# Score pieces in pairs, batch exponentials and separate message tiles in two edge-attention loops

## The chip, the cores and the metric

The kernel runs on one core of a Trainium2 chip. The time is the device time of one execution in microseconds (us); the kernel before has a median of 6476.23 us over four runs (6473.66 to 6476.97). A core has five engines with an instruction stream each: TensorE (PE, matrix products), VectorE (DVE), ScalarE (ACT), GpSimd (POOL) and SyncE (SP). Here POOL issues the gathers (indirect DMAs, one row of a table for each of 128 partitions) and SP the plain DMAs.

## The reference, cut to what matters

A graph network with two attention layers, each followed or preceded by dense layers:

```python
x = x + gat(layernorm(x))             # 6250 nodes, 206250 edges, 4 heads of 64
x = x + mixture_of_experts(layernorm(x))
x = x + weighted_neighbour_sum(layernorm(x))
x = x + gat_routed_ffn(layernorm(x))  # 131072 edges, 4 heads of 4, then 4 experts
# both attentions, for each edge (src, dst) and each head:
e = leaky_relu(a_src[src] + a_dst[dst], 0.2)
p = exp(e - segment_max(e, dst)[dst])
out = segment_sum(p / segment_sum(p, dst)[dst] * h[src], dst)
```

Both attentions run through one function, `gat_stream`. Edges are sorted by destination.

## The kernel before

**Tiles, pieces, batches.** 128 edges, one per partition, make an edge tile. Q = 8 edge tiles make a piece, PB = 4 pieces (B = 32 edge tiles) a batch. The first attention has 1612 edge tiles, that is 202 pieces (the last has 4 tiles) in 51 batches; the second has 787, that is 99 pieces (the last has 3) in 25 batches. `DH` is the width of a message (256 and 16), `H` = 4 the heads, `W = DH + 2 * H`. `parts` is 1 in the first attention and 3 in the second, where messages are split into three bf16 terms. `s.group` is 16 in the first and None in the second.

**One loop, written out by hand.** `gat_stream` ends with a loop over steps `s_` under a manual schedule: instructions stand on each engine in the order in which the loop writes them, and each engine takes its own in order. In step `s_` with `k = s_ - 2` and `q = s_ - 10` the loop writes:

- `gathers(s_)` (L1303): eight indirect DMAs on POOL, one for each edge tile, into a tile `g` of the piece, which holds the message part h[src] and a_src[src]. Of these tiles there are 13 in the first attention and 14 in the second.
- `load(s_ + 3)` (L1279, L1285), every fourth step: the destinations of a batch, spread over all partitions (`db`, two tiles of 8 KB a partition), and the marks `kf` of where a destination starts. On SP.
- what is left of earlier nodes: `done` (L1974 to L1994 in the first attention), then `normed`, `twice`, `logits` in later steps.
- `scores(k)` (L1333 to L1343): DVE sums three terms of a_dst (`nd`, from a PSUM tile `pds` with two halves, one for even and one for odd pieces), adds a_src out of `g`, takes the leaky relu, subtracts the node's own score and writes `Z`. The add is the first instruction that waits for the gathers of piece k to land.
- `turned_hots(k + 3)` (L1313): DVE compares `db` with the node numbers; `node_parts(k + 2)` (L1324): PE picks a_dst with it, into the half of `pds` that `scores(k)` has just read.
- `greatest`, `turn_scores`, `turn_back` once a batch: two scans on DVE (L1355, L1358) find the greatest score of each destination, PE turns the tile before and after.
- `weights(i)` (L1374 to L1379), once a batch, when `k % 4 == 3`: ACT takes the exponentials of the whole batch into `ps[0]`; then, for each of the four pieces, ACT takes them again into columns DH to DH + H of the piece's `g`, and DVE writes the product of the maximum and the end mark `il` into the last H columns.
- `one_hots(q + 1)` (L1184) and `messages(q + 1)` (L1386): DVE multiplies the message part by the exponentials, in place in `g`. In the second attention it then makes the three bf16 terms (L1391, L1393).
- `sums(q, 0)` and `sums(q, 1)` (L1409): PE adds up the messages of each destination; it reads `g` itself in the first attention, which frees the tile of piece q at step q + 10.

**Around it.** The first attention's result goes to a routed layer whose expert products (L634, L647) fill the middle of the span; the weighted neighbour sum with its own gathers (L234) follows; the second attention comes last, and the kernel ends with its last nodes.

## Time and profile before

| what | value |
|---|---|
| median of four runs | 6476.23 us |
| profiled execution, its own time | 6479.13 us |
| its span | 6477.3 us |
| first attention's gathers, first issue to last end | 192.87 to 2241.08 us |
| weighted sum's gathers (L234) | 1616 of 947 ns |
| second attention's gathers, first issue to last end | 5390.06 to 6394.25 us |
| PE, DVE, ACT, POOL busy over the span | 59%, 67%, 19%, 63% |

Busy shares over the whole span mix stages with different limits; what a change in one stage is worth is read in a window of that stage. In a line of the timeline, the first number is the start in us and the second the duration; what stands in square brackets is how long the engine was idle before, and what ended the wait. A group's line ends with busy time, mean duration of one in ns, and the idle time before its instructions with what ended it. "issue" means that the engine waited for nothing that the profile shows.

### The profile page before, as it was taken

To read this page: it belongs to the slowest core of one execution; us is meant where nothing else is said; L and a number is where in the kernel's file an instruction comes from. 1 tells how busy PE (TensorE), PEld (TensorE's weight loads), DVE (VectorE), ACT (ScalarE), POOL (GpSimd) and SP (SyncE) were. 2 spreads that over 40 slices of the span, in tenths; PEclk is the share of its full clock that TensorE was granted. 3 is DMA by queue.
4 is the path that set the end of the run, shared out by engine and by line. 5 is a ranking of instruction groups with operands and counts; after the bars stand their busy time and mean duration, and the time that the engine had idled before them with its cause. 6 is when DMAs were issued, how large, how long until landed. Compare 5 with 4: busy or idle time off the path is not lost.

```text
span 6477.3 us, 61956 instructions
## 1 busy us (share of the span) xinstructions
PE 3819.2 (59%) x17583; PEld 2863.5 (44%) x17583; DVE 4330.1 (67%) x10445; ACT 1204.2 (19%) x2770; POOL 4094.1 (63%) x4304
## 2 busy tenths in 40 slices
PE   4266666666666679999514777776777677111111
PEld 3144444444445458888402444444444445111111
DVE  5266666666666683444368888888888872777777
ACT  2011111112221112333100222222222222000000
POOL 0677777777777612232147777777777765777773
PEclk9678777778877789999755888888888888555555
DMA  4644555554545425557563444444444443233332
GB/s 131 142 146 145 146 147 147 146 146 146 146 145 146 112 97 196 187 185 235 182 213 112 128 126 129 129 128 125 129 128 127 126 118 83 53 76 76 76 76 56
DMA packets 495996, 856.25 MB, mean 132 GB/s; under 512 B 140311, under 2 KB 345304, under 8 KB 486135
## 3 DMA queue, kind: packets, MB, share of 16 engines
q0 software_dynamic: 190112, 461.21, 26.8%
q1 hardware_dynamic: 280226, 366.94, 17.3%
q10 hardware_dynamic: 25300, 24.00, 1.1%
q8 instruction: 143, 2.34, 0.2%
q14 instruction: 215, 1.75, 0.1%
HBM read 758.44 MB, written 95.50 MB: 132 GB/s over the span
## 4 chain that ended last, share of the span: by engine, by line
POOL 33%; DVE 18%; issue 17%; PE 16%; DMA 15%; ACT 1%; DVEq 0%; SPq 0%; ACTq 0%; POOLq 0%; another core or an unknown queue 0%
POOL g L234 17%; POOL g L1303 16%; DMA g<-tab,si 7%; PE py L647 5%; PE ph L634 5%; DMA g<-tab_ef,si 3%; DVE g L1386 3%; DVE run L2102 3%; PE acc L1409 2%; DMA g<-tab_1f,si1s 2%; DVE oh L1184 2%; DMA xc<-x_d 1%; DVE ot L1313 1%; PE bacc L1435 1%; DVE R L1355 1%
## 5 line engine op out<-in xcount | busy, mean ns | idle before, releaser
L234 POOL DMA_INDIRECT g<-tab_ef,si x1616 | 1530.9, 947 | 618.6 <-issue 590.5
L1303 POOL DMA_INDIRECT g<-tab,si x1612 | 1557.4, 966 | 505.1 <-issue 411.9
L2102 DVE SCALAR_TENSOR_TENSOR run<-g,wab,run 128x256 f32<-128x256 f32 x2626 | 1264.1, 488 | 328.1 <-DMA g<-tab_ef,si 248.5
L1409 PE MATMUL acc<-g,oh 128*128 128x264 f32 x3224 | 1013.9, 468 | 309.5 <-DVE g L1386 242.8
L1409 PEld LDWEIGHTS acc<-g,oh 128*128 128x128 f32 x3224 | 726.3, 234 | 492.5 <-DVE g L1386 272.2
L1303 POOL DMA_INDIRECT g<-tab_1f,si1s x787 | 764.6, 972 | 250.3 <-issue 213.3
L2219 PE MATMUL acc<-run,oh 128*128 128x256 f32 x808 | 302.5, 511 | 689.7 <-DVE oh L2106 534.0
L1335 DVE TENSOR_TENSOR z<-g,nd 128x32 f32<-128x32 f32 (+1 forms) x301 | 58.0, 193 | 841.9 <-DMA g<-tab,si 687.9
L1409 PE MATMUL acc<-s,oh 128*128 128x72 bf16 x1267 | 106.4, 249 | 751.5 <-DVE s L1391 751.5
L2219 PEld LDWEIGHTS acc<-run,oh 128*128 128x128 f32 x808 | 190.3, 251 | 792.6 <-issue 468.5
L1772 PE MATMUL pf<-xt,w 128*128 128x512 f32 (+1 forms) x832 | 410.9, 627 | 98.5 <-ACT h L1777 98.4
L1386 DVE TENSOR_TENSOR g<-g,mix 128x2048 f32<-128x2048 f32 x202 | 458.9, 2272 | 0.0
L1409 PEld LDWEIGHTS <-oh 128*128 128x128 bf16 x1267 | 85.8, 127 | 763.1 <-issue 480.6
L1784 PE MATMUL pf<-w,h 128*128 128x256 f32 x1568 | 403.4, 401 | 0.0
L634 PE MATMUL ph<-xe,w 128*128 128x256 f32 x1664 | 377.1, 383 | 4.9 <-DVE xe L622 4.9
L647 PE MATMUL py<-w,h 128*128 128x256 f32 x1664 | 370.0, 380 | 0.0
L610 POOL DMA_INDIRECT xg<-tab_x,gi x104 | 117.8, 1133 | 351.9 <-PE pt L619 278.6
L634 PEld LDWEIGHTS ph<-xe,w 128*128 128x128 f32 x1664 | 316.7, 192 | 48.3 <-DVE xe L622 5.9
L1784 PEld LDWEIGHTS pf<-w,h 128*128 128x128 f32 x1568 | 289.7, 195 | 100.3 <-issue 67.0
L647 PEld LDWEIGHTS py<-w,h 128*128 128x128 f32 x1664 | 312.4, 191 | 40.1
L650 POOL DMA_INDIRECT tab_y<-y,so x104 | 111.9, 1076 | 267.9 <-DVE y L649 263.4
L1772 PEld LDWEIGHTS pf<-xt,w 128*128 128x128 f32 x832 | 164.2, 210 | 247.8 <-issue 124.4
(510 smaller groups left out, 6076.4 us busy)
## 6 DMA issues: line engine op xcount, KB each, us to landing
w<-in_L_ffn_W SPq DMA_DIRECT2D x104, 1024.0 KB
db<-s_d SPq DMA_DIRECT2D x74, 1024.0 KB
yb<-y_d SPq DMA_DIRECT2D x49, 640.0 KB
g<-tab_ef,si POOLq DMA_INDIRECT x1616
g<-tab,si POOLq DMA_INDIRECT x1612
y_d<-y SPq DMA_DIRECT2D x196, 128.0 KB
g<-tab_1f,si1s POOLq DMA_INDIRECT x787
yy<-tab_y SPq DMA_DIRECT2D x7, 1792.0 KB
```

The lines of the kernel that those rows point to most:

```text
L234: nc.gpsimd.indirect_dma_start(out=dst, out_offset=None, in_=table, in_offset=bass.IndirectOffsetOnAxis(ap=si[:, t:t + 1], axis=0))
L610: nc.gpsimd.indirect_dma_start(out=xg[:, i, :], out_offset=None, in_=tab_x, in_offset=bass.IndirectOffsetOnAxis(ap=gi[:, 2 * j + i:2 * j + ...
L634: nc.tensor.matmul(ph, w1[:, k, f * P:(f + 1) * P], xe[:, k, :], start=(k == 0), stop=(k == KD - 1))
L647: nc.tensor.matmul(py, hs[f][:, i * P:(i + 1) * P], w2[:, f, :], start=(f == 0), stop=(f == FC - 1))
L1184: nc.vector.tensor_tensor(o[:, :m], ips[:, None, k * P:(k + 1) * P].to_broadcast([P, m, P]), dl[:, a:a + m, None].to_broadcast([P, m, P]), ...
L1303: nc.gpsimd.indirect_dma_start(out=g[:, j, :DH + H], out_offset=None, in_=tab, in_offset=bass.IndirectOffsetOnAxis(ap=si[:, t0 + j:t0 + j ...
L1386: nc.vector.tensor_mul(gh, gh, ps[0][:, o:o + n, :, None].to_broadcast([P, n, H, CD]))
L1409: nc.tensor.matmul(acc[b].rearrange("p s w -> p (s w)"), oh[:, t - a], m_, start=(t == lo), stop=(t == hi))
L1772: nc.tensor.matmul(ph[:, :n], w1[:, e, k, f * P:(f + 1) * P], xts[g][:, k, :n], start=(k == 0), stop=(k == KD - 1))
L1784: nc.tensor.matmul(py[:, :D], hs[g, e, f][:, j * P:(j + 1) * P], w2[:, e, f, :], start=False, stop=(f == FC - 1))
L2102: nc.vector.scalar_tensor_tensor(at[:, i] if j < Q - 1 else r[i], g[:, j, :], w, at[:, i], op0=OP.mult, op1=OP.add)
L2219: nc.tensor.matmul(acc[i], oh[:, k], r[k], start=(q % 2 == 0 and k == 0), stop=(last and k == 1))
```

## The change

- **Messages of the first attention.** `g` loses the columns for the maxima (260 columns in place of 264) and has 11 tiles in place of 13. `messages` writes the product into a new tile `m` (264 columns, 3 tiles), an ACT copy puts the exponentials and maxima into its last 8 columns, and `sums` reads `m`. The tile `g` is so free after `messages`, at step q + 9.
- **Exponentials and maxima of a batch.** `weights` makes one exponential and one DVE product for the whole batch, in a tile `pw`. In the second attention four ACT copies a batch bring them into the pieces; in the first, the copies in `messages`.
- **Scores for two pieces.** At even k, `scores` takes pieces k - 1 and k together: one reduction over both halves of `pds`, an add for each piece, one leaky relu, a subtraction for each piece. A last piece that is not full is taken alone, and so is the piece before it in that step.
- **Order.** `turned_hots` runs two pieces ahead in place of three and `node_parts` one in place of two. In the first attention `load` brings two pieces at a time (`LB = 2`, 4 KB a partition, still two tiles), so that `load(q)` has to wait until `turned_hots(q - 3)` has read the tile.

```diff
--- before.py
+++ after.py
@@ -1236,6 +1236,7 @@
         PB = B // Q
         nbatch = -(-npiece // PB)
         LAG = 10
+        LB = 2 if s.group else PB
         with ExitStack() as st:
             pool = lambda name, bufs, **k: st.enter_context(tc.tile_pool(name=f"{s.name}_{name}", bufs=bufs, **k))
             gp = pool("gs", 1)
@@ -1273,11 +1274,11 @@
                 return Z[i]
 
             def load(q):
-                if q % PB == 0:
-                    n = min(PB * Q, T - q * Q) * P
-                    d = mp.tile([P, PB * Q * P], I16, name="db", bufs=2)
+                if q % LB == 0:
+                    n = min(LB * Q, T - q * Q) * P
+                    d = mp.tile([P, LB * Q * P], I16, name="db", bufs=2)
                     nc.sync.dma_start(d[:, :n], s.d16[q * Q * P:q * Q * P + n][None, :].to_broadcast([P, n]))
-                    for k in range(PB):
+                    for k in range(LB):
                         dbs[q + k] = d[:, k * Q * P:(k + 1) * Q * P]
                 if q % PB == 0:
                     i = q // PB
@@ -1298,7 +1299,7 @@
 
             def gathers(q):
                 t0, n = span(q)
-                g = piece[q] = mp.tile([P, Q, W], F32, name="g", bufs=13 if parts == 1 else 14)
+                g = piece[q] = mp.tile([P, Q, DH + H if parts == 1 else W], F32, name="g", bufs=11 if parts == 1 else 14)
                 for j in range(n):
                     nc.gpsimd.indirect_dma_start(
                         out=g[:, j, :DH + H], out_offset=None, in_=tab,
@@ -1325,22 +1326,25 @@
                                          nbw[b] if s.group else NB[:, b].rearrange("p s d -> p (s d)"),
                                          start=(k == 0), stop=(k == len(use) - 1))
 
-            def scores(q):
-                t0, n = span(q)
-                pd = pds[:, q % 2]
-                g = piece[q]
-                nd = mp.tile([P, Q, ND], F32, name="nd")
-                nc.vector.tensor_reduce(nd[:, :n], pd[:, :n].rearrange("p j s d -> p j d s"), AX.X, OP.add)
-                z = mp.tile([P, Q, H], F32, name="z")
-                nc.vector.tensor_add(z[:, :n], g[:, :n, DH:DH + H], nd[:, :n, :H])
-                nc.vector.scalar_tensor_tensor(z[:, :n], z[:, :n], 0.2, z[:, :n], op0=OP.mult, op1=OP.max)
-                i, o = divmod(t0, B)
-                zb = z_of(i)
-                nc.vector.tensor_sub(zb[:, 1 + o:1 + o + n, :], z[:, :n], nd[:, :n, H:])
-                if o == 0 and i > 0:
-                    nc.scalar.copy(Z[i - 1][:, B + 1, :], zb[:, 1, :])
-                if o + Q == B and i + 1 < nbatch:
-                    nc.scalar.copy(z_of(i + 1)[:, 0, :], zb[:, B, :])
+            def scores(qs):
+                lo, hi = min(q % 2 for q in qs) * Q, max(q % 2 * Q + span(q)[1] for q in qs)
+                nd = mp.tile([P, 2 * Q, ND], F32, name="nd")
+                nc.vector.tensor_reduce(nd[:, lo:hi], pds.rearrange("p k j s d -> p (k j) d s")[:, lo:hi], AX.X, OP.add)
+                z = mp.tile([P, 2 * Q, H], F32, name="z")
+                for q in qs:
+                    o, m = q % 2 * Q, span(q)[1]
+                    nc.vector.tensor_add(z[:, o:o + m], piece[q][:, :m, DH:DH + H], nd[:, o:o + m, :H])
+                nc.vector.scalar_tensor_tensor(z[:, lo:hi], z[:, lo:hi], 0.2, z[:, lo:hi], op0=OP.mult, op1=OP.max)
+                for q in qs:
+                    t0, n = span(q)
+                    k = q % 2 * Q
+                    i, o = divmod(t0, B)
+                    zb = z_of(i)
+                    nc.vector.tensor_sub(zb[:, 1 + o:1 + o + n, :], z[:, k:k + n], nd[:, k:k + n, H:])
+                    if o == 0 and i > 0:
+                        nc.scalar.copy(Z[i - 1][:, B + 1, :], zb[:, 1, :])
+                    if o + Q == B and i + 1 < nbatch:
+                        nc.scalar.copy(z_of(i + 1)[:, 0, :], zb[:, B, :])
 
             def turn_scores(i):
                 zf = Z.pop(i).rearrange("p t h -> p (t h)")
@@ -1372,27 +1376,34 @@
                 if i == 0:
                     ps[0] = gp.tile([P, B, H], F32, name="pe") if pe is None else pe
                 nc.scalar.activation(ps[0], pb[:, 0], AF.Exp)
-                for q in range(i * PB, min((i + 1) * PB, npiece)):
-                    t0, n = span(q)
-                    o = t0 - i * B
-                    nc.scalar.activation(piece[q][:, :n, DH:DH + H], pb[:, 0, o:o + n], AF.Exp)
-                    nc.vector.tensor_tensor(piece[q][:, :n, DH + H:], pb[:, 1, o:o + n],
-                                            il[:, t0:t0 + n, None].to_broadcast([P, n, H]), op=OP.mult)
+                pw = ps[1] = mp.tile([P, B, 2 * H], F32, name="pw")
+                nc.scalar.activation(pw[:, :, :H], pb[:, 0], AF.Exp)
+                nb = min(B, T - i * B)
+                nc.vector.tensor_tensor(pw[:, :nb, H:], pb[:, 1, :nb],
+                                        il[:, i * B:i * B + nb, None].to_broadcast([P, nb, H]), op=OP.mult)
+                if parts > 1:
+                    for q in range(i * PB, min((i + 1) * PB, npiece)):
+                        t0, n = span(q)
+                        o = t0 - i * B
+                        nc.scalar.copy(piece[q][:, :n, DH:], pw[:, o:o + n])
 
             def messages(q):
                 t0, n = span(q)
                 i, o = divmod(t0, B)
                 gh = piece[q][:, :n, :DH].rearrange("p n (h c) -> p n h c", h=H)
-                nc.vector.tensor_mul(gh, gh, ps[0][:, o:o + n, :, None].to_broadcast([P, n, H, CD]))
+                pe_ = ps[0][:, o:o + n, :, None].to_broadcast([P, n, H, CD])
                 g = piece.pop(q)
-                if parts > 1:
+                if parts == 1:
+                    m = split[q] = mp.tile([P, Q, W], F32, name="m", bufs=3)
+                    nc.vector.tensor_tensor(m[:, :n, :DH].rearrange("p n (h c) -> p n h c", h=H), gh, pe_, op=OP.mult)
+                    nc.scalar.copy(m[:, :n, DH:], ps[1][:, o:o + n])
+                else:
+                    nc.vector.tensor_mul(gh, gh, pe_)
                     s3 = split[q] = mp.tile([P, Q, parts, W], BF, name="s3", bufs=3)
                     for k in range(parts):
                         nc.vector.tensor_copy(s3[:, :n, k], g[:, :n])
                         if k + 1 < parts:
                             nc.vector.tensor_sub(g[:, :n], g[:, :n], s3[:, :n, k])
-                else:
-                    split[q] = g
 
             def sums(q, part):
                 t0, n = span(q)
@@ -1441,11 +1452,11 @@
             with tc.manual_schedule():
                 if s.group:
                     load_nodes()
-                load(0)
-                for q in range(min(3, npiece)):
+                for q in range(0, 3, LB):
+                    load(q)
+                for q in range(min(2, npiece)):
                     turned_hots(q)
-                for q in range(min(2, npiece)):
-                    node_parts(q)
+                node_parts(0)
                 zts, dMs, pzs = {}, {}, {}
                 last, s_, later = max(npiece + LAG, PB * nbatch + 7) + 1, -1, []
 
@@ -1457,7 +1468,7 @@
                     s_ += 1
                     if s_ < npiece:
                         gathers(s_)
-                    if PB <= s_ + 3 < npiece:
+                    if LB * (2 // LB + 1) <= s_ + 3 < npiece:
                         load(s_ + 3)
                     beside()
                     now, later[:] = list(later), []
@@ -1467,19 +1478,24 @@
                         b = ready.pop(0)
                         follow(done(b, sums_of.pop(b), items.pop(b), mp))
                     k, q = s_ - 2, s_ - LAG
-                    if 0 <= k < npiece:
-                        scores(k)
+                    if 0 <= k < npiece and (k % 2 == 0 or k == npiece - 1):
+                        pair = [k - 1, k] if k % 2 == 0 and k > 0 else [k]
+                        if span(k)[1] == Q:
+                            scores(pair)
+                        else:
+                            for p in pair:
+                                scores([p])
                     i = k // PB - 1
                     at = k % PB if 0 <= i < nbatch else None
-                    if 3 <= k + 3 < npiece and k >= 0:
-                        turned_hots(k + 3)
+                    if 2 <= k + 2 < npiece:
+                        turned_hots(k + 2)
                     beside()
                     if 0 <= q < npiece:
                         sums(q, 0)
                     if at == 2:
                         pzs[i] = turn_back(*dMs.pop(i))
-                    if 0 <= k and k + 2 < npiece:
-                        node_parts(k + 2)
+                    if 0 <= k and k + 1 < npiece:
+                        node_parts(k + 1)
                     move_sums()
                     if at == 1:
                         dMs[i] = greatest(i, zts.pop(i))
```

## The prediction

> **What bounds the kernel now.** I read the page first, then the groups of POOL, then the waits and the windows of the two attentions, last the timeline of single gathers and of the two tails. The page, with POOL's busy tenths in 40 slices and the chain that ended last:
>
> ```profile
> span 6477.3 us, 61956 instructions
> POOL 0677777777777612232147777777777765777773
> ...
> POOL 33%; DVE 18%; issue 17%; PE 16%; DMA 15%; ACT 1%; DVEq 0%; SPq 0%; ACTq 0%; POOLq 0%; another core or an unknown queue 0%
> ```
>
> POOL shows a steady 7 in both attentions (slices 2 to 14, 34 to 39), and POOL with "issue" is half of the chain. A 7 looks like slack; the groups of POOL over the whole span say that it is not:
>
> ```profile
> L1303 POOL DMA_INDIRECT g<-tab,si x1612 | 1557.4, 966 | 505.1 <-issue 411.9 <-DVE Z L1339 27.7 <-PE acc L1409 16.4
> L234 POOL DMA_INDIRECT g<-tab_ef,si x1616 | 1530.9, 947 | 618.6 <-issue 590.5 <-DVE run L2102 25.6 <-DMA g<-tab_ef,si 1.8
> L1303 POOL DMA_INDIRECT g<-tab_1f,si1s x787 | 764.6, 972 | 250.3 <-issue 213.3 <-DMA g<-tab_1f,si1s 11.9 <-DMA vec<-in_L_ffn_ln_gamma 10.7
> ```
>
> In the first attention 1557.4 busy and 505.1 idle, less 14.2 before the first gather, are 2048.2 us: all of 192.87 to 2241.08. The idle time is 0.30 us before each gather. The waits of the first attention from 300 to 2200 us (total, times, longest):
>
> ```profile
> DVE z L1335 <- DMA g<-tab,si: 624.0, 157, 7.4
> ...
> POOL g L1303 <- issue: 377.8, 1240, 0.3
> ```
>
> No wait of POOL is longer than 0.3: it never waits for a buffer, it goes from gather to gather, and DVE waits for what it brings. The second attention is the same (764.6 and 250.3, less 10.7 before the first, are its 1004.2 us). The windows of both (columns: length, then busy time of PE, PEld, DVE, ACT, POOL):
>
> ```profile
> 192.00:2242.00 2050.00, 1235.10 (x5598) 946.86 (x5599) 1239.99 (x2471) 333.78 (x807) 1557.39 (x1612) 0.76 0.51 146
> 5389.00:6395.00 1006.00, 231.29 (x2831) 183.52 (x2832) 712.88 (x2252) 95.08 (x297) 764.64 (x787) 0.54 0.30 74
> ```
>
> DVE works 6.1 us a piece (1240/202) against POOL's 10.2 in the first, 7.2 (712.9/99) against 10.2 in the second. So DVE counts in two places only: where it stretches a gather, and in the tails behind the last gather (2241 to 2300, 6394 to 6477). A stretch, from the timelines of POOL and DVE:
>
> ```profile
> 255.81 0.99 POOL L1303 DMA_INDIRECT g<-tab,si  x1 [0.30 <-issue]
> 257.11 1.22 POOL L1303 DMA_INDIRECT g<-tab,si  x1 [0.30 <-issue]
> 258.63 0.94 POOL L1303 DMA_INDIRECT g<-tab,si  x1 [0.30 <-issue]
> ...
> 256.88 0.69 DVE L1358 TENSOR_TENSOR_SCAN M<-kf,R 128x256 f32<-128x256 bf16 x1
> ```
>
> The gather that begins while the scan M runs takes 1.22 us in place of 0.94. Against the 947 ns of L234, all stretches together cost (966-947) x 1612 = 31 us and (972-947) x 787 = 20 us: 51 us.
>
> **The change, part by part.**
>
> Batch exponentials and products. First attention: out go 202 exponentials (196 ns, L1378) and 202 products (192 ns, L1379, with 0.30 us of waiting before each: 59 us); in come 51 exponentials of 128 columns (0.26, L1374), 51 products (nearest row L1361, 128x128: 0.29) and 202 copies on ACT (nearest L1378, about 0.2, 40 us). DVE is relieved of 39 + 59 - 15 = 83 us less some 15 of remaining waits, about 68. Second: 99 products of 0.19 with 19 us of waits become 25 of 0.29: about 28 us. ACT has room (334 us of 2050, 95 of 1006). Price on the path: nothing, since POOL's gathers cover it; without that cover it would be a gain of up to 96 us.
>
> Scores in pairs. A reduction of 96 columns takes 0.23 and of 192 takes 0.34; by that slope one of 384 takes 0.56 (an estimate; bounds 0.34 and 0.68), 0.12 less than two. The leaky relu of 32 columns takes 0.19, of 64 perhaps 0.23: 0.15 less. So 0.27 us a pair, 27 us and 13 us, under the same cover. What it moves: the adds of an odd piece now stand behind the landing of the next, even piece, while the rest of the odd step runs without waiting. DVE's work of two steps, 12.2 us in the first, has to fit into 20.3.
>
> Order and loads. `node_parts(k)` now comes one step before its scores. In that step DVE has at least a one-hot (1.22) and messages (2.28) to do, PE four passes of sums and the products, about 2 us: no wait in the first attention. At the start of the second, PE is full with leftover expert work and DVE waits for it already (53.1 us in 7 waits); POOL kept going there, and its 14 tiles leave four pieces of room. The loads: the halved `db` waits on SP for the comparison of its own step; behind it on SP stand the rows for `done` (two steps early or more) and stores that nobody awaits here. From issue to landing the first 1 MB load took 6 us (203.5 to 209.6), half of it should take no longer, and it is wanted three steps later, over 20 us. Cost nothing; uncovered, each microsecond late costs up to 101 us.
>
> Here a rule speaks against the change. The Trainium skill ("DMA: Bandwidth & Descriptors", Bandwidth) says to batch transfers to 1 MiB or more, because of a fixed part of about 2 us in each; 50 more loads would by that cost 100 us of queue time. The trace hides loads altogether, so the sum by the trace stays as it is.
>
> Tiles. POOL's gather p + 11 needs `messages(p)`, at step p + 9. At the latest DVE begins that step when piece p + 7 has landed, up to 4.7 us after its last issue, and has up to 10 us to do; POOL comes to p + 11 three pieces, 30 us, after that issue. Some 15 us remain. `m` has three tiles for a reader one step behind. Cost nothing.
>
> Stretches. The trace of before can't show how the new order meets the gathers. Bounds: all 51 us vanish, or they double. The instructions that stretch (comparisons, scans, the five of `done`) stay in number and length; the pair drops 101 and 49 leaky relus, but puts the comparison of an even step about 0.2 us later against the gathers and frees that of the odd step from its phase. I take 0, the row as it is, and keep +-51 for the range.
>
> The skill's page "SBUF — State Buffer" (Who interferes with whom) says that a DVE instruction with two SBUF inputs blocks a GpSimd instruction that reads SBUF until it ends. Row 257.11 agrees. If each of the 150 leaky relus gone had blocked for its whole 0.19 us, the sum would be 29 us lower; by the rows most gathers that run beside such short ones take 0.95.
>
> Tails. First attention, the batch at 2261 (ACT, then DVE):
>
> ```profile
> 2261.12 0.26 ACT L1374 ACTIVATE mix<-zt 128x128 f32<-128x128 f32 x1
> ...
> 2261.52 0.19 DVE L1379 TENSOR_TENSOR g<-zt,il 128x32 f32<-128x32 f32 x1 [2.18 <-ACT g L1378]
> ...
> 2262.99 2.28 DVE L1386 TENSOR_TENSOR g<-g,mix 128x2048 f32<-128x2048 f32 x1
> ```
>
> From the exponential to messages 1.87 us; with two exponentials (starts 0.18 apart) and one product it is about 0.7: -1.2, and -0.3 in the last batch. Against it the add and subtraction of piece 199 come behind the last wait (+0.4), and PE waits for the copy behind messages once on the chain (+0.2). Together -0.9. Second attention: four products from 6417.1 to 6418.6 become one (-1.2), three at 6438.1 likewise (-0.7); the scores of piece 95 (+0.3) and a late comparison (+0.2) come behind the last wait: -1.4.
>
> Sum: 6479.1 (the profiled execution: span 6477.3 and 1.8 around it) - 0.9 - 1.4 + 0 = 6476.8. That execution is 2.9 us above the median of the runs shown, so I predict **6474**.
>
> **The rivals.**
>
> (1) Slower: POOL gets to wait. Mechanism: the `db` load, held on SP until DVE's comparison, lands after it is wanted, DVE falls behind and the 11 tiles run out. It decides from a load of about 20 us, against 6 seen. At 0.4 us late in each of 101 loads: +40, 6514. For it: SP now meets DVE in each pair. Against: no wait of POOL at all before.
>
> (2) Slower: the new phase stretches more; the comparison of the even step begins just ahead of the next gather. Half of 51 more: 6500.
>
> (3) Faster: the phase goes the other way, half of the stretches vanish: 6449.
>
> (4) Faster: DVE is the bound after all. Then 68 + 27 us and 28 + 13 us come off the span: 6338, or 6433 if only in the second. Against it stand the 0.3 us of all POOL's waits.
>
> (5) The change doesn't do what it says at the ends: the second attention's last pieces (97 and 98) are not paired. That is in the sum.
>
> **How the numbers follow.** My case 0.63 (own range 6463 to 6487, a quarter of the stretches either way), (1) 0.08, (2) 0.11, (3) 0.14, (4) 0.04. A measurement tells about 0.2% (13 us) from no change. Faster: (3), (4) and an edge of mine, 0.19; slower: (1), (2) and none of mine, 0.19; same 0.62. For eight in ten I leave out (1), (4) and the far ends of (2) and (3): 6446 to 6504.
>
> **What would show it.** Right: POOL's groups again with 0.30 us before each gather and means within 10 ns of 966 and 972; one product a batch; DVE's busy time in the first window lower by some 50 us without effect; the wait of the adds on the gathers, 624 us, longer. Wrong: a wait of POOL over 0.3 us for DVE (case 1), means of gathers beyond 980 or under 955 (cases 2 and 3), or windows of the attentions shorter by more than the means explain (case 4).

## The result, and the profile after

The changed kernel takes 6489.33 us (median of 36 runs, 6483.49 to 6495.72) against 6476.96 us of the kernel before (56 runs, 6469.43 to 6489.77), a ratio of 1.0019 with a 95% interval of 1.0015 to 1.0024. It is slower by 12 us; I had forecast no change, at 6474. Five of the six chips of the experiments run the kernel before itself in 7619 to 7683 us and not in 6477 (mean granted TensorE clock 0.72 there, 0.77 on the sixth and in the profiles before and after), so each total below is compared with the kernel before on the same chip.

The page of the changed kernel (span, then the chain by engine):

```profile
span 6483.7 us, 60642 instructions
...
POOL 40%; issue 19%; DVE 16%; PE 13%; DMA 11%; ACT 1%; DVEq 0%; ACTq 0%; SPq 0%; POOLq 0%
```

The groups of POOL, and the add of the scores (busy time, mean ns of one, idle time before them and what ended it):

```profile
L1304 POOL DMA_INDIRECT g<-tab,si x1612 | 1577.5, 979 | 505.1 <-issue 475.5
L1304 POOL DMA_INDIRECT g<-tab_1f,si1s x787 | 759.5, 965 | 250.3 <-issue 212.4
...
L1336 DVE TENSOR_TENSOR z<-g,nd 128x32 f32<-128x32 f32 (+1 forms) x301 | 58.0, 193 | 981.6 <-DMA g<-tab,si 786.6
```

POOL's idle time before the first attention's gathers is 505.1 us, as before. The whole loss of that stage is in the mean: 979 ns in place of 966, 20.1 us more busy time. The second attention's mean falls from 972 to 965 ns. The first attention's waits from 300 to 2200 us (total, times, longest) and the same window as was shown of before:

```profile
POOL g L1304 <- issue: 435.9, 1431, 0.3
...
DVE z L1336 <- DMA g<-tab,si: 715.4, 101, 9.6
```

```profile
192.00:2242.00 2050.00, 1199.17 (x5543) 912.75 (x5543) 1168.23 (x2101) 326.33 (x842) 1562.84 (x1597) 0.76 0.52 144
```

No wait of POOL is over 0.3 us: 11 tiles are enough here. DVE has 72 us less to do in this window (1168.23 against 1239.99), which cuts off the end of the longer stage; over the whole stage, to 2261 us, it is 60 less (1179.4 against 1239.2). It waits for the gathers instead: 715 us against 624. So everything that the change saved on DVE became waiting, and 20 us came in where DVE stretches gathers. By stage, from the first start to the last end of the gathers (us; the last two columns are experiments told below):

| stage | before | after | k_dvecopy | k_early |
|---|---|---|---|---|
| first attention's gathers | 2048.2 | 2068.2 | 2045.0 | 2035.4 |
| from there to the first gather of the weighted sum | 1063.1 | 1058.5 | 1062.0 | 1060.8 |
| weighted sum's gathers | 2022.8 | 2024.0 | 2024.7 | 2024.1 |
| from there to the second attention's first | 63.0 | 59.6 | 59.8 | 59.2 |
| second attention's gathers | 1004.2 | 999.1 | 998.9 | 1000.2 |
| from its last gather to the end | 83.1 | 81.4 | 81.0 | 83.2 |
| span | 6477.3 | 6483.7 | 6463.8 | 6455.4 |

The profiled executions differ by 6.4 us, the medians by 12.4: the one before lies 2.2 over its median, the one after 3.7 under. Rows 2 to 4 move by 5 us and less, also in k_early, which changes nothing there, so I read nothing from them.

**Which instruction stretches.** "The comparison" is what `turned_hots` does on DVE (L1313 before, L1314 after). Each gather of the first attention that takes over 961 ns is put to the DVE instruction that runs 60 ns after the gather's start; the table sums what these gathers take over 946 ns (us):

| running on DVE | before | after | k_dvecopy | k_early |
|---|---|---|---|---|
| comparison (L1313, L1314), behind scores | 11.5 | 18.8 | 18.5 | 2.1 |
| comparison, odd step without scores | none | 10.6 | 3.8 | none |
| second scan (M) | 8.8 | 10.9 | 6.5 | 10.7 |
| closing of a window, in `done` | 11.1 | 12.6 | 0.0 | 1.8 |
| others | 1.7 | 0.6 | 0.7 | 5.6 |
| all | 33.1 | 53.5 | 29.5 | 20.2 |

Of the 20 us, 18 are the comparison's. (Of the 5.6 in k_early's "others", 3.3 are the comparison's too, in another way; see there.) Its two places in the timeline of the changed kernel, first an even step, then an odd one (start, duration):

```profile
1024.91 0.19 DVE L1336 TENSOR_TENSOR z<-g,nd 128x32 f32<-128x32 f32 x1 [9.05 <-DMA g<-tab,si]
1025.13 0.22 DVE L1337 SCALAR_TENSOR_TENSOR z<-z 128x64 f32<-128x64 f32 x1
1025.39 0.29 DVE L1343 TENSOR_TENSOR Z<-z,nd 128x32 f32<-128x32 f32 x2
1025.60 0.48 DVE L1314 TENSOR_SCALAR ot<-db,s_nid 128x1024 bf16<-128x1024 int16 x1
1025.76 1.15 POOL L1304 DMA_INDIRECT g<-tab,si  x1 [0.30 <-issue]
...
1032.44 0.46 DVE L1314 TENSOR_SCALAR ot<-db,s_nid 128x1024 bf16<-128x1024 int16 x1
1032.51 1.21 POOL L1304 DMA_INDIRECT g<-tab,si  x1 [0.30 <-issue]
```

and a step of the kernel before:

```profile
1046.79 0.19 DVE L1335 TENSOR_TENSOR z<-g,nd 128x32 f32<-128x32 f32 x1 [5.48 <-DMA g<-tab,si]
1047.01 0.19 DVE L1336 SCALAR_TENSOR_TENSOR z<-z 128x32 f32<-128x32 f32 x1
1047.24 0.19 DVE L1339 TENSOR_TENSOR Z<-z,nd 128x32 f32<-128x32 f32 x1
1047.35 0.48 DVE L1313 TENSOR_SCALAR ot<-db,s_nid 128x1024 bf16<-128x1024 int16 x1
1047.58 1.07 POOL L1303 DMA_INDIRECT g<-tab,si  x1 [0.30 <-DVE Z L1339]
```

The add is released by a landing, so everything behind it stands at a fixed distance from POOL's gathers. Before, the comparison starts 0.56 us behind the add and 0.23 us ahead of the next gather, which takes 1.07. After, a wider leaky relu and a second subtraction lie between: 0.69 us behind the add, 0.16 ahead of the gather, which takes 1.15.

**The law.** I took each comparison's lead (how long before a gather's start it starts) and that gather's time over 946 ns; the rows are the means of that time over 946 ns, for comparisons of 470 to 490 ns in both attentions:

| lead, ns | 0-50 | 50-100 | 100-150 | 150-200 | 200-250 | 250-300 | 300-350 | 350-400 |
|---|---|---|---|---|---|---|---|---|
| kernel before alone | | 258 | 230 | 176 | 121 | 73 | 27 | -1 |
| before, after, k_dvecopy, k_early | -1 | 264 | 223 | 180 | 127 | 74 | 29 | -1 |
| 14 runs with the same comparison on four other chips | 3 | 258 | 222 | 178 | 127 | 80 | 26 | 0 |

The stretch is about 325 ns less the lead, from a lead of 50 to 325, and nothing under 50 and from 350 to 400. A comparison that starts behind the start of a running gather is another case; k_early shows it. In the steps whose add waited over 0.15 us for a landing, the comparison's median lead was 298 ns before and 155 after; the mean stretch went from 67 (168 such steps) to 190 ns (99).

### The profile page after: what moved, and what is told of

Its sections match the earlier page's. It is cut to its first block, busy times and chain, and to the rows that moved or that the text cites. A ratio compares the mean times of both kernels' runs of the same rounds, so it can differ in the third digit from the quotient of the medians.

```text
span 6483.7 us, 60642 instructions
## 1 busy us (share of the span) xinstructions
PE 3799.7 (59%) x17583; PEld 2841.3 (44%) x17583; DVE 4239.4 (65%) x9924; ACT 1211.2 (19%) x2846; POOL 4110.4 (63%) x4304
## 4 chain that ended last, share of the span: by engine, by line
POOL 40%; issue 19%; DVE 16%; PE 13%; DMA 11%; ACT 1%; DVEq 0%; ACTq 0%; SPq 0%; POOLq 0%
POOL g L1304 23%; POOL g L234 17%; PE ph L634 5%; PE py L647 5%; DMA g<-tab_ef,si 3%; DMA g<-tab,si 3%; DMA g<-tab_1f,si1s 2%; DVE run L2118 2%; DVE oh L1184 2%; DVE m L1398 1%; DVE ot L1314 1%; DMA xc<-x_d 1%; DMA tab_y<-y,so 1%; PE pf L1788 1%; DVE s L1404 1%
## 5 line engine op out<-in xcount | busy, mean ns | idle before, releaser
L1304 POOL DMA_INDIRECT g<-tab,si x1612 | 1577.5, 979 | 505.1 <-issue 475.5
L1420 PE MATMUL acc<-m,oh 128*128 128x264 f32 x3224 | 1038.5, 477 | 393.3 <-DVE rd L1990 228.5
L1420 PEld LDWEIGHTS acc<-m,oh 128*128 128x128 f32 x3224 | 739.1, 239 | 579.0 <-issue 392.3
L1398 DVE TENSOR_TENSOR m<-g,mix 128x2048 f32<-128x2048 f32 x202 | 459.0, 2272 | 0.0
L637 ACT ACTIVATE h<-ph,pa 128x256 f32<-128x256 f32 x416 | 196.8, 473 | 397.2 <-PE ph L634 396.3
```

What stands on the lines that cost most here:

```text
L637: nc.scalar.activation(h, ph, AF.Gelu, bias=pa[:, f:f + 1])
L1304: nc.gpsimd.indirect_dma_start(out=g[:, j, :DH + H], out_offset=None, in_=tab, in_offset=bass.IndirectOffsetOnAxis(ap=si[:, t0 + j:t0 + j ...
L1398: nc.vector.tensor_tensor(m[:, :n, :DH].rearrange("p n (h c) -> p n h c", h=H), gh, pe_, op=OP.mult)
L1420: nc.tensor.matmul(acc[b].rearrange("p s w -> p (s w)"), oh[:, t - a], m_, start=(t == lo), stop=(t == hi))
```

## The experiments

**Theories.** A: the phase, that is where between two gathers the comparison starts, as above; 18.8 us come from the even step's comparison. B: the message tiles, their copies or the batch weights. C: the halved loads. D and E came up on the way.

**One half of the change each, and the comparison's place.** All four on one chip, before 7682.99 us.

e1_pairs is the kernel before with the pairs, the order and the loads, e2_tiles with the rest and the loads:

```
 e1_pairs  + scores([k - 1, k]) ... turned_hots(k + 2) ... node_parts(k + 1); LB = 2
 e2_tiles  + m, pw, 11 g tiles of 260 columns; LB = 2
```

> Three theories. A (phase): of the 20 us that the first attention's gathers take longer, 18.8 come from the comparison of the even step, which now starts behind two additions, a leaky relu and two subtractions instead of one each, and so is still running when the next gather starts. B (tiles): the cost comes from the message tiles, their copies on ACT or the batch weights. C (loads): it comes from the halved index loads. This kernel is the one before with the pairs of scores, the new order of the comparisons and node products, and the halved loads; tiles and weights are as before. A: mean of the first attention's gathers 977 to 981 ns, time 6482 to 6492 us. B: mean 966 ns, time 6477 us. C: as A.

> The kernel before with the other half of the change: message tiles, their copies on ACT, weights by batch, and the halved loads; scores are of one piece at a time, in the old order. A: mean of the first attention's gathers 964 to 968 ns, time 6472 to 6478 us. B: mean about 979 ns, time 6489 us. C: as B.

Measured: e1_pairs 7710.43 us, 1.0039 (1.0012 to 1.0066); e2_tiles 8054.95 us, 1.0481 (1.0448 to 1.0515). Mean gather 960 and 961 ns. Neither fits A or B as I had put them: on this chip POOL has waits that it never had in the profiles before and after. From e1_pairs, 300 to 2300 us:

```profile
POOL g L1304 <- issue: 422.1, 1219, 3.9
POOL g L1304 <- ACT lo L735: 78.0, 20, 5.3
...
POOL g L1304 <- PE zt L1353: 29.3, 1, 29.3
```

With such waits on POOL, DVE seldom waits for a landing (29 steps of e1_pairs, none of e2_tiles), the phase is loose, and a total says nothing of 12 us. What can be used of these chips is the gathers themselves. All stretches of the first attention sum to 24.1 us in e1_pairs and 25.2 in e2_tiles, but those by the comparison to 13.4 and 4.3; of these the odd steps without scores give 7.9 and 0.3. So the odd step's part of the loss comes with the pairs and their order, and neither with the tiles and weights (B) nor with the halved loads (C), which both kernels have. The even step's part, 5.5 against 4.0, isn't told apart on this chip.

e3_early is the changed kernel with the comparison moved ahead:

```
                 nc.vector.tensor_add(z[:, o:o + m], ...)        # both adds of the pair
+            turned_hots(k + 2)
             nc.vector.scalar_tensor_tensor(z[:, lo:hi], ...)
```

> The changed kernel with the even step's comparison issued right behind the second addition, ahead of the leaky relu and the two subtractions; nothing else differs. A: the comparison runs from about 0.5 to 1.0 us after a gather's start and is over when the next one starts at 1.25; its 18.8 us of stretches fall under 3, the 10.4 us of the odd steps (comparison behind the steps of a closing window) stay, mean of the first attention's gathers 967 to 971 ns, time 6467 to 6473 us. B and C: as the changed kernel, 979 ns and 6489 us.

Measured 7990.51 us, 1.0403 (1.0371 to 1.0435). The total is no answer, and the forecast for the stretches failed: those by the comparison behind scores sum to 10.0 us and not to under 3. On this chip the adds start anywhere between two gathers, and with them the comparison. An add waited for a landing in 11 steps only; there the stretch is 9 ns on average (190 in the profile after).

e4_late puts a short copy ahead of the comparison in the kernel before:

```
+                        nc.vector.tensor_copy(idle[:, :128], ips[:, :128])
                         turned_hots(k + 3)
```

> The kernel before with one short copy (128 by 128, from PSUM) put on VectorE ahead of each step's comparison; it does nothing but make the comparison start about 0.2 us later. A: in the first attention some 200 comparisons that stretch a gather by 57 ns on average would stretch it by 200 to 260: +30 to +42 us there, mean of the gathers 985 to 992 ns; second attention 0 to +20; time 6505 to 6540 us. If it is only VectorE's load that counts, or if the delay is covered: 6477 to 6480 us. B and C say nothing of it but 6477.

Measured 7664.08 us, 0.9970 (0.9951 to 0.9990), mean gather 960.5 ns. The forecast of +30 to +42 us failed. No add is put down to a landing, so no phase is known; the comparison's stretches sum to 8.4 us, against 4.3 in e2_tiles, which has the same order without the copy. That is A's sign and far from the size that I forecast; it decides nothing.

**The comparison without the shared operand.** The node numbers are copied to PSUM once:

```
-                    nc.vector.tensor_scalar(o[:, :m * P], db[...], nid[:, b:b + 1], None, op0=OP.is_equal)
+                    nc.vector.tensor_tensor(o[:, :m * P], db[...],
+                                            ips[:, 2 * P + b:2 * P + b + 1].to_broadcast([P, m * P]), op=OP.is_equal)
```

> The changed kernel with the comparison of indices with node numbers reading its node numbers from PSUM (a tensor-tensor comparison with one operand in SBUF) instead of SBUF. In the traces an instruction of VectorE with an operand in PSUM never stretched a gather. A (phase of the comparison against the gathers): the comparison takes about 1.2 us instead of 0.48, but its stretches, 29 us in the first attention and 9 in the second, are gone; mean of the first attention's gathers 959 to 963 ns, of the second's 953 to 957; time 38 us below the changed kernel. B and C: gathers as in the changed kernel, time the same or above, since VectorE has 290 us more to do.

Measured 7962.57 us in one run (before 7643.51). The changed kernel did not run on this chip, so the 38 us by which this should beat it have nothing to be compared with. In the same phase as the step shown of the changed kernel:

```profile
425.86 1.21 DVE L1315 TENSOR_TENSOR ot<-db,ips 128x1024 bf16<-128x1024 int16 x1
426.01 0.95 POOL L1305 DMA_INDIRECT g<-tab,si  x1 [0.30 <-issue]
```

A lead of 153 ns, and the gather takes 0.95. No comparison of this form stretched a gather by over 15 ns in the first attention. All stretches there sum to 12.7 us, against 22.1 in e3_early. So the stretch belongs to the operand or the mode of the comparison, not to DVE being busy. The mean of the first attention is 956 ns, under the forecast of 959 to 963; that of the second, 955, is in its range.

**Taking TensorE out, to get the old regime back.** In e1_pairs DVE waits for TensorE's results where it had waited for landings, so I took late results of TensorE for what holds these chips.

> The kernel before without some seven in ten of the matmuls of the weighted sums (those of the tiles that are no multiple of four and neither first nor last of a window), so that TensorE is not waited for on a chip where its matmuls come slower; the other engines do all that they did. It is the base of the three beside it, and all are compared by the time from the first to the last gather of the first attention, 2048 us in the profile before and 2068 in the profile after. If TensorE was all that held this chip back: 2040 to 2060 us, mean gather 964 to 968 ns.

> The changed kernel with the same matmuls left out. All theories: the first attention's gathers 18 to 22 us longer than in the thinned kernel before, mean 977 to 981 ns, if TensorE no longer holds them; the second attention's 3 to 7 us shorter.

> The kernel before with the pairs of scores, the new order and the halved loads, but the old tiles and weights; the same matmuls left out. A (phase): as thin_after, first attention 2064 to 2070 us, mean gather 976 to 981 ns. B (tiles, copies, batch weights): as thin_before, 2048 us, 966 ns. C (loads): as thin_after.

> The changed kernel with the even step's comparison right behind the second addition; the same matmuls left out. A: the 18.8 us of stretches by the even step's comparison fall under 3, first attention 2046 to 2054 us, mean gather 966 to 971 ns. B and C: as thin_after, 2068 us, 979 ns.

Measured (before 7683.10): 7724.58, 7964.78, 7725.50 and 7969.24 us, the first attention's gathers 2340, 2594, 2331 and 2618 us (2353 in k_before11 below, with all its matmuls). So it isn't the amount of TensorE's work. The totals can't be set against the whole kernel: with sums left out the routed layer gets other routes, 112 gathers in place of 104, and that stage takes 816 us in place of 723. The forecasts for the stretches failed as well: those by the comparison behind scores sum to 4.8 us in thin_after, 0.8 in thin_pairs and 5.0 in thin_early, where A asked for some 18, some 18 and under 3. Few adds waited for a landing here (10, 15 and 21 steps), so these four decide nothing about A.

> The kernel before with all of TensorE's matmuls left out of both attentions (node products, transposes of scores and maxima, weighted sums and their moves; their PSUM tiles are filled once), and all that VectorE, ScalarE, GpSimd and SyncE do there kept. It is the base for the two beside it; what is compared is the time from the first to the last gather of the first attention (2048 us, mean gather 966 ns in the profile before) and which instruction of VectorE stretches gathers. If TensorE's late results are what makes the chips of these runs slower: 2040 to 2055 us, mean 962 to 968 ns.

> The changed kernel with the same left out. All theories: gathers stretched as in the profile after, first attention's mean 976 to 981 ns, 16 to 22 us longer than nope_before; of the difference the comparison accounts for 15 us or more.

> The kernel before with the pairs of scores, the new order of comparisons and node products and the halved loads, but the old tiles and weights; the same matmuls left out. A (phase of the comparison): as nope_after, mean 975 to 981 ns, 14 to 22 us longer than nope_before. B (message tiles, their copies, batch weights): as nope_before, within 4 us and 3 ns. C (halved loads): as nope_after, but without more stretches by the comparison.

Measured in one run each (before 7659.11): 7548.56, 7469.79 and 7493.36 us; first attention 2308, 2274 and 2281 us, mean 959, 960 and 964 ns; stretches by the comparison 6.3, 7.1 and 7.8 us. The forecasts of 2040 to 2055 us and of 15 us more by the comparison failed, again because POOL waits. One face of what holds these chips shows in nope_before, where nothing of TensorE stands in the way:

```profile
1004.48 0.19 DVE L1334 TENSOR_TENSOR z<-g,nd 128x32 f32<-128x32 f32 x1
1004.71 0.19 DVE L1335 SCALAR_TENSOR_TENSOR z<-z 128x32 f32<-128x32 f32 x1
...
1029.54 0.19 DVE L1334 TENSOR_TENSOR z<-g,nd 128x32 f32<-128x32 f32 x1 [2.31 <-DMA g<-tab,si]
1030.92 0.19 DVE L1335 SCALAR_TENSOR_TENSOR z<-z 128x32 f32<-128x32 f32 x1 [1.19 <-DVE z L1334]
1032.32 0.19 DVE L1338 TENSOR_TENSOR Z<-z,nd 128x32 f32<-128x32 f32 x1 [1.21 <-DVE z L1335]
```

An instruction that needs the one before it on its own engine starts 0.23 us behind it in one step and 1.4 us in another. Up to 2500 us DVE waits so for itself 200 times in nope_before, but not once in e1_pairs and once in k_before11, which have it 170 and 163 times in later stages. So it isn't what holds the first attention of the whole kernels; what does, I don't know.

**Tiles on these chips** (before 7619.41). e2_tiles, e3_early and e5_psum, all with 11 tiles, were some 4 per cent slower, so D: the number of tiles.

```
 k_after     the changed kernel
 k_before11  - bufs=13   + bufs=11
 k_before14  + LB = 2, bufs=14
 k_best14    k_before14, the comparison of e5_psum, and
-                R = mp.tile([P, 3 * P], F32, name="R")
+                R = zt.rearrange("p k e -> p (k e)")      # d is taken from a copy of zt[:, 1]
```

> The changed kernel itself, on the chips of these runs, on which semaphores and with them free tiles come later than in the profile before, so that POOL waits for tiles. D (tiles): as the other kernels with 11 gather tiles, 3.5 to 4.8 per cent slower than the kernel before, 7950 to 8060 us. A alone (phase of the comparison): 0.2 to 0.4 per cent.

> The kernel before with 11 gather tiles in the first attention instead of 13, nothing else. D: 3.5 to 4.8 per cent slower, as the changed kernel. If it is the message tiles' copies, the pairs or the new order: as before within 0.3 per cent.

> The kernel before with halved index loads and, in the room that this frees, 14 gather tiles instead of 13. D: faster by up to 2 per cent, half of what the two tiles cost, POOL's waits in the first attention shorter by 50 to 150 us. If 13 are enough: as before within 0.3 per cent.

> The same with 14 tiles, the comparison reading its node numbers from PSUM, and the first scan of the maxima writing over its input in PSUM, so that the second scan has one operand in SBUF. A: the comparison and the scans stretch no gather in either attention (20 to 30 us in the profiles before and after); D: POOL waits as in k_before14. Time 0.2 to 0.5 per cent under k_before14 where POOL does not wait, less where it does; VectorE has some 440 us more to do.

Measured: k_after 7930.10 us, 1.0393 (1.0345 to 1.0441); k_before11 7611.38, 0.9975 (0.9951 to 0.9998); k_before14 7629.32, 1.0007 (0.9983 to 1.0031); k_best14 7708.15, 1.0115 (1.0075 to 1.0155). D falls: two tiles fewer cost nothing, one more gains nothing, and the halved loads of k_before14 cost nothing either. All kernels here with message tiles and weights by batch are 3.5 to 4.8 per cent slower, and none without them is slower by more than 1.2. With TensorE left out it is not so (nope_after was faster than nope_before, one run each). That and the second row below, of e2_tiles' waits from 300 to 2200 us, speak for E: TensorE waits for ACT's copy into `m`, while ACT stands behind a copy that waits for TensorE.

```profile
PE acc L1417 <- issue: 434.1, 41, 30.9
PE acc L1417 <- ACT m L1396: 387.8, 15, 34.8
```

k_best14 has stretches of 9.3 and 6.5 us left in the two attentions (k_before14: 13.9 and 16.5), none by the comparison or a scan. It is slower all the same; DVE is busy for 253 us more (4606.3 against 4353.1, not the 440 of the forecast), and I take this for the cause without having tried it.

**The two runs that decide.** They ran on the sixth chip (before 6477.10 us), where POOL doesn't wait.

```
 k_early (the kernel before)
                 nc.vector.tensor_add(z[:, :n], g[:, :n, DH:DH + H], nd[:, :n, :H])
+                turned_hots(k + 3)                     # was behind the subtraction
                 nc.vector.scalar_tensor_tensor(z[:, :n], z[:, :n], 0.2, ...)
 k_dvecopy (the changed kernel)
-                    nc.scalar.copy(m[:, :n, DH:], ps[1][:, o:o + n])
+                    nc.vector.tensor_copy(m[:, :n, DH:], ps[1][:, o:o + n])
```

> The kernel before with the comparison issued right behind the addition of the scores, ahead of the leaky relu and the subtraction; same instructions, same tiles. A: a comparison that waits with its addition for a landing starts some 0.1 us behind it, 0.6 to 0.8 us ahead of the next gather, and stretches none: 0 to 10 ns each there, against 84 in the profile before; stretches of the first attention by the comparison under 3 us. Time on these chips the same within their spread, 0.3 per cent.

> The changed kernel with the copy of a piece's weights behind its messages made by VectorE instead of ScalarE; nothing else differs. E (the copy on ScalarE couples TensorE to ScalarE's queue): TensorE's waits on it (230 us and much of the 530 us beside it) go, and the 3.9 per cent with them: within 0.7 per cent of the kernel before. If it is the message tiles or the weights by batch themselves: 3 to 4 per cent slower, as the changed kernel. A says nothing of it: the comparison's phase stays, about 200 ns a stretch.

k_early: 6460.19 us, 0.9977 (0.9967 to 0.9987), 16.9 us faster than the kernel before with the same instructions on the same tiles. A step of it, and its gathers:

```profile
1023.71 1.03 POOL L1303 DMA_INDIRECT g<-tab,si  x1 [0.30 <-issue]
1024.03 0.19 DVE L1335 TENSOR_TENSOR z<-g,nd 128x32 f32<-128x32 f32 x1 [4.62 <-DMA g<-tab,si]
1024.14 0.48 DVE L1313 TENSOR_SCALAR ot<-db,s_nid 128x1024 bf16<-128x1024 int16 x1
1024.54 0.18 DVE L1337 SCALAR_TENSOR_TENSOR z<-z 128x32 f32<-128x32 f32 x1
1024.76 0.19 DVE L1340 TENSOR_TENSOR Z<-z,nd 128x32 f32<-128x32 f32 x1
...
1025.05 0.95 POOL L1303 DMA_INDIRECT g<-tab,si  x1 [0.31 <-DVE Z L1340]
```

```profile
L1303 POOL DMA_INDIRECT g<-tab,si x1612 | 1544.6, 958 | 505.2 <-issue 413.7 <-DVE ot L1313 18.6 <-PE acc L1410 17.7
```

The comparison starts 0.11 us behind the add and is over before the next gather. In the 176 steps whose add waited for a landing it stretched the next gather by 9 ns on average (67 before), and the sum fell from 11.5 to 2.1 us.

That has a price, for the comparison now starts while a gather is running. Where it starts 350 to 475 ns behind that gather's start, the gather is stretched, like the one of 1023.71: 34 times, by up to 126 ns, 3.3 us in all. Where it starts 475 to 700 ns behind, the gather takes its 0.95 and the comparison takes longer, up to 0.72 us, as here, 0.50 behind a gather's start:

```profile
1031.85 0.69 DVE L1313 TENSOR_SCALAR ot<-db,s_nid 128x1024 bf16<-128x1024 int16 x1
```

95 comparisons of the first attention take 653 ns on average in place of 480. These 16 us fall on DVE, which has them to spare.

The stage is 12.8 us shorter: 9.4 by the comparison ahead of a gather and 9.3 by the closing of windows (11.1 to 1.8), which the shift moved as well, less 3.9 in "others" (3.3 of them the price just told) and 1.9 at the scan. The second attention gives 4.0 more. I had expected the totals not to show it, on the other chips; here they do. For the comparison A is shown in both directions: later in the step it stretches more, earlier it stretches less. The changed kernel with only its even step's comparison moved did not run on this chip.

k_dvecopy: 6466.31 us, 0.9986 (0.9977 to 0.9995), against 1.0019 of the changed kernel. It was meant to test E, which needs a chip where POOL waits; so E stays open. I read it as phase again; that ACT is relieved of the copies is not told apart from it. One more short instruction per step on DVE:

```profile
1040.11 0.18 DVE L1399 COPY m<-pw 128x64 f32<-128x64 f32 x1
1040.21 0.48 DVE L1314 TENSOR_SCALAR ot<-db,s_nid 128x1024 bf16<-128x1024 int16 x1
1040.48 1.01 POOL L1304 DMA_INDIRECT g<-tab,si  x1 [0.30 <-issue]
```

The even step's comparison, tied to the landing, stretches as in the changed kernel (18.5 against 18.8 us). What follows the messages is moved by 0.1 to 0.2 us: the odd step's comparison falls from 10.6 to 3.8 us, the closing of windows from 12.6 to none, the scan from 10.9 to 6.5. 36 us more of DVE's work in that attention (202 copies of 0.18) went with a first attention 23 us shorter than the changed kernel's.

## Why the prediction was wrong

- **What bounds the kernel: right.** POOL's idle time is 505.1 us in the first attention before and after, 0.30 before each gather; the means explain the whole of both stages.
- **Batch weights, pairs, order, loads: right as terms of 0 on the path.** DVE lost 60 us over the first attention (I had said some 50) and waited 91 us longer for the gathers. The pair's reduction took 0.52 to 0.55 us (forecast 0.56). No load held POOL up.
- **Tiles at no cost: right where the prediction was made.** On the chips with late signals the message tiles or the batch weights cost 3.5 to 4.8 per cent; the number of `g` tiles doesn't. The prediction did not have that case.
- **The term that failed: "Stretches", "I take 0".** It measured +20.4 us in the first attention (33.1 to 53.5) and -5.2 in the second (21.5 to 16.3). The step gave its own reason: "the comparison of an even step about 0.2 us later against the gathers". It was 0.135 later behind the add and 0.14 against the gathers (median leads of 298 and 155 ns), and that alone is the even step's +7 us in half as many steps. For the odd step, "frees that of the odd step from its phase" was taken as neutral; it came to stand behind the closing of a window with a lead of some 70 ns, where a stretch is longest: +10.6.
- "The trace of before can't show how the new order meets the gathers" was the mistake behind it. The law stands in the trace of before, in its row of the table above. With it, 0.135 us later in 99 steps that start at a lead of 298 ns is 99 x 0.135 = 13 us more than as many steps had, by working (12 us measured: 99 x (190 - 67) ns). The neutral value had no row to speak for it.
- **Rival (2) is what happened**, by its mechanism; in size about half: 20 us in the first attention, less the 5 that the second gave back, where I had 26 for both. By my own signs it fell between: a mean of 979 ns is more than 10 off 966 and not beyond 980. I had given it 0.11, against 0.14 for the opposite, with no argument between the two. And 12 us, which I had taken for no measurable change, lie clear of the spread with 56 and 36 runs.
- **Tails.** The second attention's was 1.7 us shorter (forecast 1.4), 2.1 in k_dvecopy and not at all in k_early, which has none of that edit. The first's 0.9 is lost in a row that moves by 4 us.
- The Trainium skill's page "SBUF — State Buffer" (Who interferes with whom) has the rule that I weighed only for the leaky relus: a `tensor_scalar` in a two-port mode, or two operands in SBUF, locks GpSimd out, and "Issue order, not op shape, decides who blocks." The runs agree on both: the comparison with a lead stretches and with one operand in PSUM does not; one that starts within 100 ns behind the gather's start stretches next to nothing (61 of them before and after: 5 ns). In k_early the order decides once more within a gather: up to 475 ns behind its start the gather waits, from there on the comparison. The page has the later one wait until the other's end. In the rows the stretch is smaller: with leads of 50 to 325 it is what of the comparison lies beyond 155 ns after the gather's start (480 - 325), and in the prediction's row 257.11, which I had called agreement, 0.27 us of the 0.46 for which the scan still ran. Why a lead under 50 costs nothing stays open.

## What to carry to other kernels

Where one engine runs without a pause and another is released by its results, a short instruction's place in the step can be worth more than its removal: here 60 us of DVE's work saved in a stage bought nothing, a move of 0.45 us bought 17 us in all. Before an edit behind such a release, bin the trace by lead (start of the one against the next start of the other), and read what a shift of the order's own 0.1 or 0.2 us would do to each instruction that shares a port. Putting the long sharing instruction first behind the release, and the short ones after it, paid here; look then at the gather that is running at that time, for the two can hold each other up there as well.

## What the runs showed of the hardware that I had not expected

- The stretch of a gather by a comparison of 480 ns falls by one ns for each ns of lead, from 264 ns at a lead of 50 to 100 to nothing at 350, the same on every chip that ran this comparison. The gather then ends some 790 ns after the comparison's end, whatever the lead (946 + 325 - 480).
- Under a lead of 50 ns the gather isn't stretched at all.
- A comparison that starts 350 to 475 ns behind a gather's start stretches that gather, by 12 ns on average at 350 to 375 and 110 at 450 to 475. One that starts 475 to 700 ns behind leaves the gather alone and is itself lengthened: it ends some 1195 ns after the gather's start, whenever it started (k_early; the runs on the other chips show the same).
- On five of six chips the kernel before took 7619 to 7683 us, with signals between and within engines some 1 us, at most 2 us, late in stretches of the stages that gather, and a mean granted clock of 0.72 in place of 0.77; which of the two brings the other, if either does, isn't shown. Leaving out seven in ten of the sums' matmuls left the first attention about as long (2340 us, 2353 in k_before11). The cause is open, and so is what in the message tiles and batch weights costs 4 per cent on them.
